# Moving squares, a copy and a norm check in a gated attention block: where they stand in the queues

## The chip, the core and the metric

The kernel runs on one core of one Trainium2 chip. The core has engines that each work through their own instructions in order: TensorE (PE in the profile; its weight loads are shown as PEld), VectorE (DVE), ScalarE (ACT), GpSimd (POOL) and SyncE (SP, which here only issues DMAs). They wait for one another through semaphores. The metric is the device time of one launch in microseconds (us); all times below are in us unless another unit is named.

## The reference

The input `x` is 32 batches of 256 rows of 256 values. Two blocks follow one another, each with a layer norm ahead of it and a gate behind it:

```
x = x + tanh(g_xattn) * xattn(layernorm(x), ctx, ctx)
x = x + tanh(g_ffn)   * ffn(layernorm(x))
```

`xattn` is an attention over 77 context rows with 8 heads, without a softmax over keys: it mixes cosine similarities with a term from variances, with weights that a small predictor computes once for the whole input. `ffn` is an attention of the 256 rows of a batch over themselves, with 16 heads, and two normalisations behind it:

```
scores = q k / sqrt(256)           (per head)
attn   = softmax(scores)
z = attn v ;  z = z @ Wo ;  z = z / max(|z|, 1e-12)
z = z @ Wff ; z = z / max(|z|, 1e-12) ;  z = gelu(z)
```

Where |z| isn't tiny, the first of the two normalisations falls out, since the second one divides by the length of every row anyway. The kernel uses that: it multiplies `Wo` and `Wff` once, and computes `u = z @ (Wo Wff)`, its rows' lengths, and gelu of the scaled rows.

## The kernel before

All arithmetic is in fp32. A preamble of about 130 us reads all of `x` once for sums over the whole input, turns the weights round and computes the predictor. Then one pass over the 32 batches follows.

**Order.** Every engine call goes through `InOrder` (line 24), which keeps the instructions of an engine in the order of the program. That order is written out by hand as lists of stages: `cycle` (line 1372), run once for each batch n from a little ahead of 0 up to 29, `last_but_one` (line 1443) for batch 30 and `last` (line 1483) for batch 31. An entry such as `(2, query_features, 0, 0)` runs that stage for batch n + 2, so a cycle works on up to seven batches at once: attention features for those ahead, the softmax of batch n, the output of batch n − 1. Two engines meet only in semaphores, which the framework sets from the tiles that are read and written. Two engines that read the same PSUM tile are ordered as well: the one that comes first in the program reads first. "Cycle n" below is the list's run for that n.

**The softmax of a batch.** It is done in four units u = 0 to 3, each of them in two halves.
- `scores(b, u)` (line 594): eight matmul instructions write scores into two PSUM buffers (pool `ps_s`, tile `sc`, two buffers, one for each half); VectorE then takes the negated maxima `nm`, one reduction for a half.
- `exponents(b, u, jp)` (line 625): four ScalarE activations for a half turn scores into `e` and add up rows into `sums`. Only then is that half's PSUM buffer free for the next unit's scores.
- `scale_values(b, u)` (line 637): VectorE takes the reciprocal of the sums and scales the values into `vz`.
- `mix_values(b, u)` (line 650): 16 matmul instructions multiply `e` and `vz` into PSUM tile `zp`. Behind unit 3, `zp` is copied to SBUF as `zT`, by VectorE (line 671). In batch 31 the copy is made in two parts, behind units 1 and 3 (line 668).

**The output of a batch.** It is done one cycle later.
- `ff_out(b)` (line 678): eight matmul instructions multiply `zT` by the joined weights into one PSUM tile of the pool `mm_tile` (line 141; three buffers, used in turn by nearly all other matmuls). ScalarE squares each half of it (tile `ge`) and adds up rows into `ny`; VectorE copies it to SBUF as `u`. In batch 31 each half has a PSUM tile of its own.
- `ff_keep` (line 704): two DMAs keep `zT` and `x` for a repair that is not needed on these inputs.
- `ff_norm_inv` (line 710): GpSimd turns `ny` into the reciprocal length `i2`.
- `ff_gelu`, `ff_add`: gelu, gate, and the DMA of the result. `ff_finish` (line 784) does all this at the end for batch 31.

**The check of the lengths.** `square_weights` (line 717) squares two weights on ScalarE, once, in cycle 4, into `bn`; its scratch tile has the tag `fb`, whose two buffers otherwise hold the transposed queries of `turn_queries` (line 470) until a DMA has read them. `bound_norms` (line 723), once, in cycle 5, sums `bn` over partitions on TensorE and makes the bound `low` of it on VectorE. `judge` (line 733), at the very end, compares all of `ny` with `low`; a repair loop, `mend`, would follow if a length were below it.

**Fillers.** `pass_time(b, n)` (line 189) issues n matmuls whose result nobody reads; the lists for the last two batches have some.

The stages around the change, as the list `cycle` has them before:

```
(-1, mix_values, 3), (0, scores, 0), ..., (0, exponents, 0, 0),
(-1, ff_out), (-1, ff_keep), (0, square_weights), (0, bound_norms),
(0, exponents, 0, 1), (2, query_features, 0, 0), (0, scale_values, 0),
(2, query_features, 0, 1), (-1, ff_norm_inv), (0, scores, 1), ...
```

Of the kernel before, what the change touches and what calls it, by code (L numbers as in the profile page):

```python
# [8 lines left out]
F32 = mybir.dt.float32  # L9
AF = mybir.ActivationFunctionType  # L10
# [4 lines left out]
P = 128  # L15
# [20 lines left out]
def gated_block_kernel(  # L36
# [25 lines left out]
    B, S, D = x.shape  # L62
    M = cx.shape[1]
    NT = S // P
# [6 lines left out]
    pa = ctx.enter_context(tc.tile_pool(name="pa", bufs=2))  # L71
# [7 lines left out]
    pe, act, dve, pool = (  # L79
        InOrder(tc, e) for e in (nc.tensor, nc.scalar, nc.vector, nc.gpsimd)  # L80
    )
# [36 lines left out]
    ny = const.tile([P, B, NT], F32, name="ny")  # L118
# [22 lines left out]
    def mm_tile():  # L141
        return ps.tile([P, 512], F32, tag="mm", name="mm")
# [60 lines left out]
    kept = [{} for _ in range(B)]  # L203
    given = set()

    def run(b, stage, *which):
        key = (b, stage.__name__, which)
        if key not in given:
            given.add(key)
            stage(b, *which)  # L210
# [439 lines left out]
    def mix_values(b, u):  # L650
        k = kept[b]
        g, kt = u // 2, u % 2
        if u == 0:
            k["zp"] = ps_z.tile([P, 2, S], F32, tag="zp", name="zp")
        es = [k.pop(("e", u, jp)) for jp in range(2)]
        for i in range(2):
            for j in range(4):
                pe.matmul(
                    k["zp"][32 * j : 32 * j + 32, g, :],
                    lhsT=vzs[u % 2][:, j, 2 * i : 2 * i + 2, :].rearrange("p i d -> p (i d)"),  # L660
                    rhs=es[j // 2][:, j % 2, i, :],
                    start=(i == 0 and kt == 0),
                    stop=(i == 1 and kt == NT - 1),
                )
        if b == B - 1 and u % 2:
            if u == 1:
                k["zT"] = pa.tile([P, 2, S], F32, tag="zT", name="zT", bufs=1)
            dve.tensor_copy(k["zT"][:, g, :], k["zp"][:, g, :])
        elif u == 3:
            zT = pa.tile([P, 2, S], F32, tag="zT", name="zT", bufs=1)  # L670
            dve.tensor_copy(zT, k.pop("zp"))
            k["zT"] = zT


# [3 lines left out]
    def ff_out(b):  # L678

        k = kept[b]  # L680
        pus = []
        for t in range(NT):
            if t == 0 or b == B - 1:
                pu = mm_tile()
            pus.append(pu[:, t * D : (t + 1) * D])
            for c in range(2):
                pe.matmul(
                    pus[t], lhsT=k["zT"][:, c, t * P : (t + 1) * P],
                    rhs=w_of[:, c, D : 2 * D], start=(c == 0), stop=(c == 1),
                )  # L690
        u = [P, NT, D], F32
        k["u"] = sw.tile(*u, tag="wf_n", name="u") if b == B - 1 else pa.tile(*u, tag="u", name="u")
        for t in range(NT):
            ge = pa.tile([P, D], F32, tag="ge", name="ge")
            act.activation(
                ge, pus[t], AF.Square, accum_out=ny[:, b, t : t + 1]
            )
        if b == B - 1:
            for t in range(NT):
                dve.tensor_copy(k["u"][:, t, :], pus[t])  # L700
        else:
            dve.tensor_copy(k["u"].rearrange("p t c -> p (t c)"), pu)

    def ff_keep(b):

        k = kept[b]
        nc.sync.dma_start(out=z_kept[:, b], in_=k["zT"])
        nc.sync.dma_start(out=x_kept[:, b], in_=k["x"])
# [12 lines left out]
                act.activation(ge, w, AF.Square, accum_out=bn[:, i : i + 1])  # L721

    def bound_norms(b):
        if b == 5:
            pt = mm_tile()
            pe.matmul(pt[:, 0:2], lhsT=ones, rhs=bn, start=True, stop=True)
            dve.tensor_copy(bn, pt[:, 0:2])
            dve.tensor_scalar(
                low, bn[:, 0:1], bn[:, 1:2], 4.0 * TINY * (S * D**0.5) ** 2, ALU.mult, ALU.mult
            )  # L730
            dve.tensor_scalar(low, low, LEAST, None, ALU.max)
# [388 lines left out]
    for g in range(NG):  # L1120
# [4 lines left out]
        for i in range(4):  # L1125
            k = 4 * g + i
# [233 lines left out]
    for pair in (2, 0, 1):  # L1360
# [11 lines left out]
    cycle = [  # L1372
        (4, load_queries),
        (-1, mix_values, 3),
        (0, scores, 0),
        (2, measure_keys),
        (2, align_keys),
        (3, norm_inputs),
        (0, exponents, 0, 0),
        (-1, ff_out),  # L1380
        (-1, ff_keep),
        (0, square_weights),
        (0, bound_norms),
        (0, exponents, 0, 1),
        (2, query_features, 0, 0),
        (0, scale_values, 0),
        (2, query_features, 0, 1),
        (-1, ff_norm_inv),
        (0, scores, 1),
        (0, exponents, 1, 0),  # L1390
        (0, mix_values, 0),
        (2, count_queries, 0),
        (2, query_features, 1, 0),
# [10 lines left out]
        (0, scores, 2),  # L1404
        (0, exponents, 2, 0),
        (0, mix_values, 1),
        (2, scale_keys),
        (1, attend, 0),
# [29 lines left out]
        (0, scale_values, 3),  # L1438
        (3, gain_inputs),
        (-1, ff_add),  # L1440
    ]

    last_but_one = [
        (-1, mix_values, 3),
        (0, scores, 0),
        (0, exponents, 0, 0),
        (-1, ff_out),
        (-1, ff_keep),
        (0, exponents, 0, 1),
        (0, scale_values, 0),  # L1450
        (1, query_ratios),
        (0, pass_time, 4),
# [36 lines left out]
        (0, exponents, 0, 0),  # L1489
        (0, exponents, 0, 1),  # L1490
        (-1, ff_out),
        (-1, ff_keep),
        (0, scores, 1, 1),
        (0, scale_values, 0),
# [14 lines left out]
        (0, exponents, 3, 0),  # L1509
        (0, mix_values, 2),  # L1510
        (0, pass_time, 5),
        (0, exponents, 3, 1),
        (0, scale_values, 3),
        (0, mix_values, 3),
# [51 lines left out]
```

## Time and profile before

| what | value |
|---|---|
| time, three runs | 1347.17, 1351.65, 1353.98 (median 1351.65) |
| the profiled execution's own time | 1349.24 |
| its span, first to last instruction | 1347.1 |
| TensorE busy | 1322.5 (98%) |
| VectorE busy | 1038.3 (77%) |
| ScalarE busy | 871.4 (65%) |
| GpSimd busy | 510.5 (38%) |
| mean granted TensorE clock | 0.997 |

A row of the timeline has the start, the duration, the engine, the line, the operation, the tiles (output <- inputs), their shape and the number of instructions merged into the row; in square brackets stands how long the engine was idle ahead of it and what ended that. The line is 32 everywhere, because all calls go through the helper `InOrder`, so one reads by the tiles' names: `sc` scores, `nm` maxima, `e` exponentials, `ge` squares, `zp` and `zT` the mixed values, `mm<-w_of,zT` the output product, `mm<-winT,xTc` query features, `vz` scaled values. A row of the waits has the engine and tile that waited, what it waited for, the total, the number of times and the longest. fp32 matmuls appear as two instructions each. The durations of matmuls are modelled and overlap, so the length of a run of matmuls is read from its start to the start of the next run.

### The profile page before, as it was taken

The numbers are of one execution on the slowest core, as the hardware profiler recorded it, in microseconds if no ns is written. First come the engines' busy times: TensorE is split into PE (matmuls) and PEld (weight loads), VectorE is DVE, ScalarE is ACT, GpSimd is POOL, SyncE is SP. The second block draws the span as 40 slices with busy tenths as digits, with TensorE's granted clock in tenths as the row PEclk, the third lists the DMA queues.
The fourth block names the chain that finished last, engine by engine and source line by source line (L and its number), as shares of the span: only waits on it lengthen the run. The fifth ranks groups of instructions, "written<-read, shape, count | busy, mean of one in ns | idle before, by whom it ended". The sixth has DMA issues, their size and how long they took to land.

```text
span 1347.1 us, 26283 instructions
## 1 busy us (share of the span) xinstructions
PE 1322.5 (98%) x8783; PEld 802.5 (60%) x8783; DVE 1038.3 (77%) x3004; ACT 871.4 (65%) x2857; POOL 510.5 (38%) x633
## 2 busy tenths in 40 slices
PE   8999999999999999999999999999999999999996
PEld 7866555666556556665556556665556565655563
DVE  6846778778788787787887787887887877878865
ACT  6822566766666767666666666666666676666666
POOL 6823344343333342435333433343433434343310
PEclk9999999999999999999999999999999999999999
DMA  8610033333233333332333333332333332422221
GB/s 275 208 32 21 28 97 116 110 115 93 70 118 113 106 116 105 117 108 88 86 114 110 115 108 116 108 101 88 101 113 106 120 101 89 134 84 68 80 86 41
DMA packets 99638, 138.25 MB, mean 103 GB/s; under 512 B 14170, under 2 KB 65039, under 8 KB 99502
## 3 DMA queue, kind: packets, MB, share of 16 engines
q1 hardware_dynamic: 98670, 136.56, 32.5%
q8 instruction: 70, 1.15, 0.3%
q14 instruction: 66, 0.54, 0.1%
q10 hardware_dynamic: 832, 0.00, 0.0%
HBM read 62.04 MB, written 64.23 MB: 94 GB/s over the span
## 4 chain that ended last, share of the span: by engine, by line
PE 91%; DVE 3%; DMA 2%; ACT 2%; POOL 1%; issue 1%; ACTq 0%; DVEq 0%; POOLq 0%; SPq 0%
PE mm L32 70%; PE sc L32 12%; PE zp L32 9%; ACT e L32 1%; DVE nm L32 1%; DMA x<-in_x_dram 1%; DMA ct<-in_ctx_dram 0%; DMA w_in_n<-in_L_xattn_w_in_dram 0%; POOL rstd_x L32 0%; DVE st L32 0%; DVE qt L32 0%; DVE qst L32 0%; DMA gcol<-in_L_xattn_ln_g_dram 0%; ACT ge L32 0%; POOL ct L32 0%
## 5 line engine op out<-in xcount | busy, mean ns | idle before, releaser
L32 ACT ACTIVATE e<-sc,nm 128x256 f32<-128x256 f32 x1016 | 467.5, 482 | 215.3 <-DVE nm L32 215.2
L32 DVE TENSOR_REDUCE nm<-sc 128x4 f32<-128x1024 f32 x254 | 298.6, 1216 | 42.8 <-PE sc L32 42.8
L32 PE MATMUL mm<-winT,xTc 128*128 128x512 f32 x512 | 234.9, 600 | 0.9 <-DVE bn L32 0.9
L32 ACT ACTIVATION_READ_ACCUMULATOR e<-sc,nm 128x1 f32 x1016 | 218.0, 215 | 0.0
L32 POOL TENSOR_TENSOR rq<-qt,nhalf 128x8 f32<-128x8 f32 x64 | 105.4, 1646 | 293.7 <-DVE qt L32 293.7
L32 PE MATMUL sc<-q,kTf 32*128 32x512 f32 x1016 | 164.0, 640 | 2.4 <-ACT e L32 1.4
L32 PEld LDWEIGHTS mm<-winT,xTc 128*128 128x128 f32 x512 | 94.0, 190 | 105.9 <-issue 102.2
L32 PE MATMUL mm<-vw,s 128*128 128x256 f32 x640 | 147.0, 384 | 0.0
L32 PE MATMUL zp<-e,vz 128*32 128x256 f32 x2048 | 137.0, 385 | 3.4 <-DVE vz L32 3.4
L32 PEld LDWEIGHTS mm<-vw,s 128*128 128x128 f32 x640 | 118.9, 190 | 28.8 <-issue 13.5
L32 POOL TENSOR_TENSOR fq<-fq,rq 128x1024 f32<-128x1024 f32 x64 | 121.4, 1896 | 5.0
L32 PEld LDWEIGHTS zp<-e,vz 128*32 128x32 f32 x2048 | 53.5, 109 | 107.5 <-issue 35.2
L32 POOL TENSOR_TENSOR nrx<-kt,nquart 128x8 f32<-128x8 f32 (+1 forms) x20 | 32.9, 1644 | 194.4 <-DVE kt L32 194.4
L32 DVE BATCH_NORM_STATS2 qst<-fq 128x6 f32<-128x128 f32 x512 | 104.6, 275 | 0.0
L32 PE MATMUL mm<-fqT,fvT 128*64 128x256 f32 (+2 forms) x1024 | 95.5, 387 | 0.0
L32 PE MATMUL mm<-woutT,fvT 128*64 128x256 f32 (+2 forms) x1024 | 93.7, 382 | 1.4 <-ACT v L32 1.4
L32 PEld LDWEIGHTS sc<-q,kTf 32*128 32x128 f32 x1016 | 48.2, 183 | 67.1 <-issue 41.0
L32 POOL TENSOR_SCALAR xn<-x,mv_x,rstd_x 128x256 f32<-128x256 f32 x64 | 80.2, 1261 | 4.2 <-issue 4.2
L32 ACT ACT_TABLE_LOAD x60 | 77.0, 1283 | 5.0 <-DMA x<-in_x_dram 4.3
L32 POOL TENSOR_SCALAR rs<-mv 128x1 f32<-128x1 f32 x64 | 14.4, 225 | 168.4 <-DVE mv L32 125.3
L32 ACT COPY fvx<-mm 128x512 f32<-128x512 f32 (+1 forms) x40 | 23.4, 585 | 80.3 <-PE mm L32 80.3
L32 PE MATMUL mm<-winT,kT_all 128*128 128x512 f32 (+1 forms) x160 | 74.9, 598 | 0.0
(232 smaller groups left out, 2160.6 us busy)
## 6 DMA issues: line engine op xcount, KB each, us to landing
fd<-fb SPq DMA_DIRECT2D x60, 512.0 KB
fqT<-fd SPq DMA_DIRECT2D x240, 128.0 KB
x<-in_x_dram SPq DMA_DIRECT2D x64, 256.0 KB
x_kept<-x SPq DMA_DIRECT2D x32, 256.0 KB
z_kept<-zT SPq DMA_DIRECT2D x32, 256.0 KB
out_dram<-x SPq DMA_DIRECT2D x31, 256.0 KB
xd<-xb SPq DMA_DIRECT2D x29, 256.0 KB
xq<-xd SPq DMA_DIRECT2D x116, 64.0 KB
```

The source lines that it names most:

```text
L32: return lambda *args, **kw: self._tc.keep_in_program_order(method(*args, **kw))
```

## The change

Five edits, four of them in the lists of stages:

1. The copy of `zp` to `zT` behind unit 3 is made by ScalarE instead of VectorE, in all batches but the last.
2. The squares of the output product are taken out of `ff_out` into a stage of their own, `ff_square`. In `cycle` and `last_but_one` it stands behind `exponents(0, 0, 1)` instead of ahead of it; in `last` it stands behind `ff_out`, where the squares were.
3. With that, VectorE's copy of the product to `u` comes ahead of the squares in the program (in batch 31 the squares stay ahead).
4. `square_weights` moves from the middle of cycle 4 to its end.
5. `bound_norms` moves from cycle 5 to the last batch, behind the second filler.

```diff
         elif u == 3:
             zT = pa.tile([P, 2, S], F32, tag="zT", name="zT", bufs=1)
-            dve.tensor_copy(zT, k.pop("zp"))
+            act.copy(zT, k.pop("zp"))
             k["zT"] = zT
...
-        for t in range(NT):
-            ge = pa.tile([P, D], F32, tag="ge", name="ge")
-            act.activation(
-                ge, pus[t], AF.Square, accum_out=ny[:, b, t : t + 1]
-            )
+        k["pus"] = pus
         if b == B - 1:
+            run(b, ff_square)
             for t in range(NT):
                 dve.tensor_copy(k["u"][:, t, :], pus[t])
         else:
             dve.tensor_copy(k["u"].rearrange("p t c -> p (t c)"), pu)
+
+    def ff_square(b):
+        for t, pu in enumerate(kept[b].pop("pus")):
+            ge = pa.tile([P, D], F32, tag="ge", name="ge")
+            act.activation(ge, pu, AF.Square, accum_out=ny[:, b, t : t + 1])
...
     def bound_norms(b):
-        if b == 5:
+        if b == B - 1:
...
         (0, exponents, 0, 0),
         (-1, ff_out),
         (-1, ff_keep),
-        (0, square_weights),
-        (0, bound_norms),
         (0, exponents, 0, 1),
+        (-1, ff_square),
         (2, query_features, 0, 0),
...
         (-1, ff_add),
+        (0, square_weights),
     ]
...
         (0, exponents, 0, 1),
+        (-1, ff_square),
         (0, scale_values, 0),
         (1, query_ratios),
...
         (-1, ff_out),
+        (-1, ff_square),
         (-1, ff_keep),
...
         (0, mix_values, 2),
         (0, pass_time, 5),
+        (0, bound_norms),
         (0, exponents, 3, 1),
         (0, scale_values, 3),
         (0, mix_values, 3),
```

## The prediction

> **What bounds the kernel now.** I read the page first: its span, its first part (busy time), its part 4 (the chain that ended last).
>
> ```profile
> span 1347.1 us, 26283 instructions
> PE 1322.5 (98%) x8783; PEld 802.5 (60%) x8783; DVE 1038.3 (77%) x3004; ACT 871.4 (65%) x2857; POOL 510.5 (38%) x633
> PE 91%; DVE 3%; DMA 2%; ACT 2%; POOL 1%; issue 1%; ACTq 0%; DVEq 0%; POOLq 0%; SPq 0%
> ```
>
> TensorE sets the end; VectorE at 77% and ScalarE at 65% have room. But a modelled busy row hides short stalls, because the modelled end of a matmul covers the wait behind it. So next I read who the weight loads (PEld) waited for: they can't start before what they wait for.
>
> ```profile
> PEld mm L32 <- DVE zT L32: 23.1, 31, 0.8
> PEld sc L32 <- ACT v L32: 12.4, 30, 0.4
> PEld sc L32 <- ACT e L32: 11.8, 31, 1.6
> ```
>
> Two of these are no stalls. After any run of eight score matmuls the loads pause 0.76, and after any mixing run 0.41, also where nothing is awaited. The third is one: score loads held, once a batch, by exponentials. The timeline of one cycle shows where:
>
> ```profile
> 601.84 1.14 PE L32 MATMUL sc<-q,kTf 32*128 32x512 f32 x8
> 602.00 0.69 DVE L32 COPY zT<-zp 128x512 f32<-128x512 f32 x1 [0.84 <-PE zp L32]
> 604.33 0.47 ACT L32 ACTIVATE e<-sc,nm 128x256 f32<-128x256 f32 x1 [2.79 <-DVE nm L32]
> 606.14 0.39 ACT L32 ACTIVATE ge<-mm 128x256 f32<-128x256 f32 x1
> 606.85 0.50 ACT L32 ACTIVATE e<-sc,nm 128x256 f32<-128x256 f32 x1
> 607.02 0.69 DVE L32 COPY u<-mm 128x512 f32<-128x512 f32 x1 [0.37 <-ACT ge L32]
> 608.20 0.52 ACT L32 ACTIVATE e<-sc,nm 128x256 f32<-128x256 f32 x1
> 608.27 1.72 PE L32 MATMUL sc<-q,kTf 32*128 32x512 f32 x8
> 608.86 0.30 PEld L32 LDWEIGHTS sc<-q,kTf 32*128 32x128 f32 x4 [0.30 <-ACT e L32]
> 609.92 1.07 PE L32 MATMUL zp<-e,vz 128*32 128x256 f32 x16
> ```
>
> The reader is to see: scores of unit 1 start at 608.27; their second half waits for the score buffer that the last exponential of unit 0 (608.20) frees. They hold TensorE until 609.92, 1.65, where the other score runs of the cycle take 1.07 (601.84 to 602.91, 617.86 to 618.93, 628.39 to 629.46). Two squares (606.14 to 606.85, 0.71) stand ahead of that last half. In all 27 ordinary cycles after the first the timeline gives 1.65 or 1.66; in the first cycle, which has no output product to square (148.75 to 149.82), 1.07. In cycle 4, where the weights' squares stand there too (299.43 to 300.66, 1.23), it is 300.85 to 303.72, 2.87: 1.22 more. So the run is late by just what stands ahead of the exponentials.
>
> **The change part by part.** Sums are against the profiled execution, 1349.24 (span 1347.1 and 2.1 around it), which is 2.4 under the median of the three runs, 1351.65.
>
> *Squares behind the second half.* The last exponential ends 0.71 earlier; the load at 608.86 could go at 608.15, before its run starts at 608.27, so the whole 0.58 is gone. 27 cycles × 0.585 = 15.8. Is the next step late? Unit 0's mixing needs the scaled values: their reciprocal starts at 608.84, now at 608.13, and the product ends 0.53 on, 608.66, against 609.34 where the mixing can start now. The output product's PSUM tile is held longer: its squares now end near 608.8. The third matmul group behind it reuses that tile, query features at 610.92, now 610.34: 1.5 of room. GpSimd's `i2` (610.50 in this cycle, behind its normalisations) gets its sums about 2 later at worst, and waits idle there in the others; its next task, `rq` at 616.19, came after 4.66 of idle. The copies of query features behind the squares start at 608.65 as before. Behind this point the other engines' work moves up with TensorE.
>
> *The order of the two readers.* VectorE's copy `u` waited for the squares (607.02, above; 28.6 in 32 waits). Now the copy is written first, so the squares wait for it; it ends near 607.4, squares start at 608.1: free. The Trainium skill, PSUM — Partial Sum Buffer, PSUM bank collisions raise a hardware error, says that ScalarE and VectorE must not read one bank together, so their reads have to be ordered; the trace agrees (607.02). If no order held, the next term would be nought. In the last batch ScalarE has no other work: copy 1323.05 to 1323.74, squares to 1324.5 instead of 1323.78, so the next exponentials start 0.7 late. Bounds: 0.7 lost, or 0.4 won, because VectorE's maxima move up from 1324.53 to 1324.1. ScalarE had 0.39 of idle at 1333.66 waiting for such a maximum; I follow the queue to there and take nought.
>
> *z copied by ScalarE.* VectorE's copy takes 0.69; ScalarE's copy of the same shape, `v<-mm`, 0.59. ScalarE's copy `v` ends at 601.54 and its next task starts at 604.33, so the new copy fits at 602.00 to 602.59, before the product's loads at 602.91. Queued behind it: those exponentials, not yet due. VectorE's maxima wait for scores (603.01) either way. Nothing on the path. In the last batch the copy ends about 1318.8 and the exponentials start there instead of 1318.46; 0.84 of idle at 1323.05 covers the 0.3.
>
> *Weights' squares at the end of cycle 4.* The 1.80 in that cycle (2.87 to 1.07) is gone. At the end `v` is copied until 333.08; squares take 1.23, and then the z copy 0.59: 334.90, for a product due at 334.45. Their scratch is the buffer of the transposed queries, read by DMAs issued at 328.98 and 330.11; the fetch behind the first started 2.67 later, so the second buffer is free by 332.8 to 333.5. Cost 0.5, bounds 0.4 and 1.2.
>
> *Norms' sum from cycle 5 to the last batch.* In cycle 5 it took a fourth PSUM tile, and query features waited: from the first scores to the second 333.38 to 341.22, 7.84, where it is 6.43 elsewhere. 1.41 gone (the 1.07 behind it stays; the 27 don't count this cycle). In the last batch the sum is queued on TensorE behind 10 filler matmuls, until 1337.51, and VectorE's three small operations behind it, ahead of unit 3's scaling, which before ran at 1335.63 and waited for nothing after. So: sum at about 1337.3, 0.3 to its end, 0.6 for the three (339.17 to 339.75), 0.6 from reciprocal to mixing: last mixing 1.5 late, less about 0.2 by which VectorE runs ahead. Cost 1.3; bounds 0.14 (the matmuls alone) and 1.7.
>
> *The cycle before the last.* Unit 1's scores took 2.92; 0.71 gone. A clock dip follows there, which the stretches show (TensorE's busy time, its clock behind POOL's):
>
> ```profile
> 1291.35:1294.76 3.41, 2.68 (x13) 0.76 (x13) 1.84 (x4) 2.19 (x11) 0.94 (x2) 1.00 0.18 67
> 1294.76:1298.17 3.41, 3.41 (x16) 1.59 (x16) 1.61 (x2) 1.57 (x6) 0.00 (x0) 0.50 0.02 5
> ```
>
> In it 16 matmuls of query scores took 3.55, elsewhere 1.88: 1.67. It is the only dip between 28 and 1346, and follows the stretch with the least work; with a shorter wait I expect it to go. Bounds 0 and 1.67; I take 1.67, as cycle 4's wait, nearly as long but followed by denser work, had no dip. The Trainium skill, TensorE: Matmul & The Clock Gate, Part 1, lets the clock drop after an idle window of about 3.4 us; the stretch ahead was busy for 2.68, so the trace differs. By that page the dip isn't tied to the wait and may stay: the sum would be 17.9.
>
> Sum: 15.8 + 1.8 − 0.5 + 1.4 − 1.3 + 0.7 + 1.7 = 19.6; 1349.2 − 19.6 = 1329.6. Three runs should lie somewhat above the profiled one, as before; half of the 2.4 makes 1331.
>
> **The rivals.**
>
> 1. *The wait moves to the PSUM tile.* If the squares end after 610.34, query features wait for the tile and part of the gain returns. For: cycle 5 shows that such a wait comes at once when a tile more is taken. Against: 1.5 of room, and nothing of VectorE's between. Half the 15.8 lost: 1339.
>
> 2. *The scores wait for something else* (a maximum's slot, a matmul), so the exchange does nothing steady. Against: 1.07 without squares, 1.22 more with 1.23 more. Only the single events remain, 1.4 net: 1348.
>
> 3. *The other side: z late on ScalarE.* It now stands at the head of ScalarE's queue before each output product. For: `q<-mm,par`, a ScalarE read of that shape, takes 0.71. Against: 0.71 still ends at 602.71. From 0.3 late TensorE waits; from 0.9 (an end at 603.5) it eats the 0.585. At 1.2 late, 29 × 0.3 = 9 slower: about 1359.
>
> 4. *The tail grows*: the last mixing 4 later instead of 1.3, for instance if a filler's tile is late too: 1334.
>
> **How the numbers follow.** Forecast 0.80, first rival 0.08, second 0.04, third 0.03, fourth 0.05. The range holds forecast and fourth rival. Down: best ends of the single events 1328, and the lowest run 2 under the profiled: 1326. Up: the dip stays, worst ends, 1333; a median 2.4 above and 2.3 of spread: 1338. About 0.5% is what a measurement of this kernel tells from no change; faster by more 0.93 (forecast, first and fourth), within 0.04, slower 0.03.
>
> **What would show it.** Unit 1's scores at 1.07 in every cycle and a cycle of about 37.2 instead of 37.74 (564.26 to 602.00, z copy to z copy); the PEld wait for `e` gone from 31 times to a few; no PEld wait on `fq` or `ge` in its place; the z copy on ScalarE ending before the product's loads; one wait of about 0.5 in cycle 5; the last mixing's loads waiting for `vz`, behind `bn`; no 0.50 clock before the end. Wrong if query features begin late behind 610, or the product's loads wait for zT by more than 0.76.

## The result, and the profile after

| | median | lowest to highest | runs |
|---|---|---|---|
| before | 1352.82 | 1347.17 to 1354.08 | 4 |
| after | 1332.51 | 1330.6 to 1335.0 | 4 |

The ratio is 0.9859, with a 95% interval of 0.9823 to 0.9895: faster by 1.4%. The forecast was 1331.0, with a range of 1326 to 1338. The profiled execution after took 1330.6 against 1349.24, 18.6 less, where the sum of the steps was 19.6.

The page of the changed kernel, by the same lines as before (span, busy time, the chain that ended last):

```profile
span 1328.6 us, 26302 instructions
PE 1303.1 (98%) x8783; PEld 793.6 (60%) x8783; DVE 1016.7 (77%) x2973; ACT 890.6 (67%) x2888; POOL 508.8 (38%) x633
PE 91%; DVE 3%; DMA 3%; POOL 1%; ACT 1%; issue 1%; SPq 0%; DVEq 0%; POOLq 0%; ACTq 0%
```

The shares hardly moved: TensorE is busy for 98% of the span and holds 91% of the chain, as before, and 19.4 of its modelled busy time is gone although it runs the same 8783 matmuls. Most of that time was a wait that the modelled ends covered; 1.67 of it was a stretch of half clock in the kernel before. VectorE lost 31 instructions and ScalarE won 31: the z copies.

One cycle in the timeline of the changed kernel (start, duration, engine, operation, tiles):

```profile
593.71 1.14 PE L32 MATMUL sc<-q,kTf 32*128 32x512 f32 x8
593.87 0.59 ACT L32 COPY zT<-zp 128x512 f32<-128x512 f32 x1 [0.46 <-PE zp L32]
594.78 1.99 PE L32 MATMUL mm<-w_of,zT 128*128 128x256 f32 x8
598.44 0.68 DVE L32 COPY u<-mm 128x512 f32<-128x512 f32 x1
599.37 0.50 ACT L32 ACTIVATE e<-sc,nm 128x256 f32<-128x256 f32 x1
599.82 0.42 ACT L32 ACTIVATE ge<-mm 128x256 f32<-128x256 f32 x1
600.14 1.14 PE L32 MATMUL sc<-q,kTf 32*128 32x512 f32 x8
600.23 0.29 DVE L32 TENSOR_TENSOR vz<-v,sums 128x128 f32<-128x128 f32 x1
601.21 1.07 PE L32 MATMUL zp<-e,vz 128*32 128x256 f32 x16
```

The reader is to see: the last exponential of unit 0 starts at 599.37, the first square only behind it at 599.82, and the scores of unit 1 take from 600.14 to 601.21, 1.07 instead of 1.65. The copy `u` (598.44) is done before the squares start. The z copy, now ScalarE's, ends at 594.46, before the product's loads. Unit 1's scores take 1.07 in every ordinary cycle, and 2.20 in the one before the last. In cycle 5 the first scores take 1.61, because z comes late there. From one z copy to the next (593.87 to 631.03) a cycle is 37.16, where it was 37.74.

A sign that was announced is missing, though. The waits of the weight loads in the changed kernel (total, times, longest):

```profile
PEld sc L32 <- ACT e L32: 23.7, 31, 1.2
PEld mm L32 <- ACT zT L32: 23.3, 30, 1.3
PEld sc L32 <- issue: 19.4, 65, 0.8
```

The wait for `e` still stands there 31 times, and longer in all than before (11.8). Yet the run of matmuls behind it is no longer late. Its 23.7 is about 31 × 0.76, the pause that the weight loads make after eight score matmuls in any case. Before, that pause stood in the row `issue`, which fell from 93 times to 65. The name moved because the exponential now ends inside the pause.

### The profile page after: what moved, and what is told of

It is laid out like the page before. It is cut to its first block, busy times and chain, and to the rows that moved or that the text cites. A ratio compares the mean times of both kernels' runs of the same rounds, so it can differ in the third digit from the quotient of the medians.

```text
span 1328.6 us, 26302 instructions
## 1 busy us (share of the span) xinstructions
PE 1303.1 (98%) x8783; PEld 793.6 (60%) x8783; DVE 1016.7 (77%) x2973; ACT 890.6 (67%) x2888; POOL 508.8 (38%) x633
## 4 chain that ended last, share of the span: by engine, by line
PE 91%; DVE 3%; DMA 3%; POOL 1%; ACT 1%; issue 1%; SPq 0%; DVEq 0%; POOLq 0%; ACTq 0%
PE mm L32 70%; PE sc L32 11%; PE zp L32 9%; DMA x<-in_x_dram 1%; DMA fd<-fb 1%; DVE nm L32 1%; DMA w_in_n<-in_L_xattn_w_in_dram 0%; DVE st L32 0%; ACT e L32 0%; DVE qt L32 0%; DVE qst L32 0%; POOL rstd_x L32 0%; DMA gcol<-in_L_xattn_ln_g_dram 0%; DVE fb L32 0%; SPq L504 0%
## 5 line engine op out<-in xcount | busy, mean ns | idle before, releaser
L32 PE MATMUL sc<-q,kTf 32*128 32x512 f32 x1016 | 147.1, 640 | 1.4 <-ACT kTf L32 1.0
L32 PEld LDWEIGHTS sc<-q,kTf 32*128 32x128 f32 x1016 | 40.2, 182 | 57.7 <-ACT e L32 23.7
```

The source lines that it names most:

```text
L32: return lambda *args, **kw: self._tc.keep_in_program_order(method(*args, **kw))
```

## The experiments

The kernel before was run again beside them: median 1349.59 (13 runs) beside the squares alone, all but the squares, the z copy put back and the first run with both checks placed; 1350.77 (one run) beside the three kernels with one run each; 1349.9 (11 runs) beside the rest.

The preamble differs from run to run: over the twelve profiled executions the first batch's output product starts at 180.79 to 183.79. So where 1 or 2 are at stake, the way from that product to the last batch's is compared. It takes 1156.25 in the kernel before and 1136.99 in the changed kernel.

### The squares alone, and all but the squares

The squares' move and the order of the two readers (edits 2 and 3) alone:

```diff
-            act.copy(zT, k.pop("zp"))
+            dve.tensor_copy(zT, k.pop("zp"))
...
-        if b == B - 1:
+        if b == 5:
...
         (-1, ff_keep),
+        (0, square_weights),
+        (0, bound_norms),
         (0, exponents, 0, 1),
...
         (-1, ff_add),
-        (0, square_weights),
...
         (0, pass_time, 5),
-        (0, bound_norms),
```

> Edits 2 and 3 alone: the squares stand behind the second half of exponentials and VectorE's copy u comes ahead of them; the z copy, the weights' squares and the norms' sum stay as before. Theory (the wait of unit 1's scores is just the ScalarE time ahead of the exponentials): 27 cycles at 1.07 instead of 1.65 (15.8 gone), cycle 4 at 2.16 instead of 2.87, the cycle before the last 0.7 less, and its clock dip gone (1.7). In cycle 5 the fourth PSUM tile now waits for squares that end later: the run of query features 5.8 instead of 4.80. Some 17.5 less than the profile of before: 1332. Rival (the z copy off VectorE brings the gain): scores stay at 1.65, time within 3 of before. Rival (the tile held): query features late in every cycle, 1339 or more.

Measured: 1333.15 (1327.79 to 1334.41), ratio 0.987 [0.9842, 0.9898]. Unit 1's scores take 1.07 in ordinary cycles and 2.14 in cycle 4, where the weights' squares still stand ahead. All of the gain that can be measured is here. One expectation failed: in cycle 5 the query features take 3.61 and nothing waits for a tile, although the norms' sum takes a fourth one; the run with later squares, below, explains that.

Edits 1, 4 and 5 without the squares' move:

```diff
         if b == B - 1:
-            run(b, ff_square)
...
+        run(b, ff_square)
+        if b == B - 1:
...
         (0, exponents, 0, 1),
-        (-1, ff_square),
```

(In all three lists the entry goes; the squares run inside `ff_out`, ahead of the copy `u`.)

> Edits 1, 4 and 5 without the squares' move: they stand between the two halves of exponentials, ahead of the copy u, as before. Theory: unit 1's scores keep 1.65 in the ordinary cycles, also in cycles 4 and 5 (2.87 and 1.07 before). Cycle 4 wins 1.2, cycle 5 1.4 less 0.6 less 0.5 for the weights' squares, the end loses 1.4: together nought, 1349 with the clock dip, 1347.5 without. Rival (the z copy on ScalarE brings the gain): 1.07, some 1332.

Measured: 1350.97 (1346.84 to 1354.3, 10 runs), ratio 1.0006 [0.9988, 1.0023]. Unit 1's scores take 1.66 or 1.67 in 28 cycles. So the other three edits together are worth less than 0.25% either way. The cycle before the last, in the timeline of this kernel:

```profile
1289.39 1.13 PE L32 MATMUL sc<-q,kTf 32*128 32x512 f32 x4
1291.26 1.13 PE L32 MATMUL sc<-q,kTf 32*128 32x512 f32 x4 [0.74 <-ACT e L32]
1292.32 2.93 PE L32 MATMUL mm<-fqT,fvT 128*64 128x256 f32 x32
```

From 1289.39 to 1292.32 the scores take 2.93, as long as before (2.92). And yet the query scores behind them run at full speed: their first 16 matmuls take 1.88, where the kernel before took 3.55 under a clock of 0.50. One row of the stretches (busy time of PE, PEld, DVE, ACT and POOL, then the clock, DMA share, GB/s):

```profile
1290.58:1294.00 3.42, 2.74 (x20) 1.36 (x20) 2.73 (x4) 1.18 (x6) 0.00 (x0) 1.00 0.02 5
```

The wait is there and the dip isn't. So the wait alone doesn't bring the dip, and the prediction's reason for its going, a shorter wait, isn't borne out. One execution can't tell whether a shorter wait makes the dip rarer.

### The z copy back on VectorE

```diff
-            act.copy(zT, k.pop("zp"))
+            dve.tensor_copy(zT, k.pop("zp"))
```

> The changed kernel with the z copy back on VectorE. Theory (that copy is off the path either way: VectorE waits for scores behind it, the product is due later): every run of matmuls of the cycles as in the changed kernel, only cycle 5 without the 0.5 in which z waited behind the weights' squares; some 0.5 less than the changed kernel, 1330. Rival (VectorE's 0.69 ahead of the maxima counts): up to 0.7 a cycle more, up to 1350.

Measured: 1332.36 (1328.56 to 1333.94), ratio 0.9867 [0.9844, 0.9891], against 0.9859 for all five edits. Up to the last batch, where this profiled execution had a stretch of half clock, the runs of matmuls are as long as in the changed kernel (within 0.3), with one exception that was expected: in cycle 5 the first scores take 1.07 instead of 1.61. Who makes this copy is of no account for the time, as the prediction had it.

### The squares split, the copy behind them, the squares later

Three kernels ask how much room the new order has. The first has one of the two squares ahead of the second half of the exponentials, and one behind:

```diff
+        (-1, ff_square, 0),
         (0, exponents, 0, 1),
-        (-1, ff_square),
+        (-1, ff_square, 1),
```

(`ff_square` takes the number of the half for this.)

> The changed kernel with one of the two squares back ahead of the second half of exponentials, the other behind. Theory (the wait is what stands ahead less the room): the second half of unit 1's scores could go 0.36 later than now, that is 0.23 late: the run takes 1.30 in the 29 cycles, 29 × 0.23 = 6.7 more than the changed kernel. Rival (a wait that comes with any square there, by the order of the readers): 1.65. Rival (all or nothing by the PSUM tile): 1.07. Here the first square also waits for VectorE's copy u, which ends about when the first half of exponentials ends or 0.7 later in cycles with key statistics; where it is later the wait grows to as much as 1.0.

Measured: 1355.19 in one run, more than in any of the 29 runs of the kernel before (at most 1354.33). Unit 1's scores take 1.29 in 10 cycles, as much as half of the squares' 0.71 would explain, but 2.42 or 2.43 in 17: a wait of 1.35, where 1.0 was expected at most. A cycle of each kind, the long one first, in the timeline of this kernel:

```profile
608.01 0.68 DVE L32 COPY u<-mm 128x512 f32<-128x512 f32 x1
608.73 0.38 ACT L32 ACTIVATE ge<-mm 128x256 f32<-128x256 f32 x1 [1.02 <-DVE u L32]
611.08 1.13 PE L32 MATMUL sc<-q,kTf 32*128 32x512 f32 x4 [0.24 <-ACT e L32]
...
645.24 0.68 DVE L32 COPY u<-mm 128x512 f32<-128x512 f32 x1
646.10 0.39 ACT L32 ACTIVATE ge<-mm 128x256 f32<-128x256 f32 x1
648.22 1.36 PE L32 MATMUL sc<-q,kTf 32*128 32x512 f32 x8
```

In the first kind ScalarE stood idle for 1.02 until VectorE had copied `u`, because VectorE first had its key statistics to do. All exponentials behind that square are late with it. In the second kind it had no such work, and nothing waits. Copy first (edit 3) thus costs nothing only while the squares stand far enough behind.

The second keeps the squares' new place, but the copy `u` comes behind them, as it did before the change:

```diff
-            dve.tensor_copy(k["u"].rearrange("p t c -> p (t c)"), pu)
+            k["pu"] = pu
...
             act.activation(ge, pu, AF.Square, accum_out=ny[:, b, t : t + 1])
+        if b < B - 1:
+            k = kept[b]
+            dve.tensor_copy(k["u"].rearrange("p t c -> p (t c)"), k.pop("pu"))
```

> The changed kernel with VectorE's copy u behind the squares again, as its second reader: the squares stand where the change put them. Theory: unit 1's scores keep 1.07, but VectorE stands waiting for the squares ahead of unit 0's scaling, so the first mixing comes about 0.8 late in each of 29 cycles: 23 more, 1354, no better than before. Rival (the order of the two readers doesn't matter): as the changed kernel.

Measured: 1354.66 in one run. Some 4.7 of it go with half clock in the last batch, of which more below (an estimate: that batch takes 5.1 more than in the changed kernel, and 0.4 of this is the order's). A cycle in the timeline:

```profile
607.90 0.43 ACT L32 ACTIVATE ge<-mm 128x256 f32<-128x256 f32 x1
608.46 0.69 DVE L32 COPY u<-mm 128x512 f32<-128x512 f32 x1 [2.19 <-ACT ge L32]
609.29 0.29 DVE L32 TENSOR_TENSOR vz<-v,sums 128x128 f32<-128x128 f32 x1
609.64 1.07 PE L32 MATMUL zp<-e,vz 128*32 128x256 f32 x16 [0.62 <-DVE vz L32]
```

VectorE waits 2.19 for the squares, and behind the copy stand the scaled values that mixing needs. From unit 1's scores to that mixing 28 cycles take 1.75 to 1.77, 0.69 more than in the changed kernel and 0.11 more than before; cycle 5 takes 1.18. That is 28 × 0.69 + 0.11 = 19.4 more than the changed kernel. Without the half clock it is about as slow as the kernel before: the squares' move without the exchange of the readers wins nothing. The exchange without the move was not run.

The third asks about the PSUM tile. The squares are put behind the first half of unit 1's exponentials, well past the 1.5 of room that the prediction gave:

```diff
         (0, exponents, 0, 1),
-        (-1, ff_square),
...
-        (-1, ff_norm_inv),
...
+        (-1, ff_square),
+        (-1, ff_norm_inv),
```

> The changed kernel with the squares (and the reciprocal length behind them) moved on behind the first half of unit 1's exponentials, some 4.5 later. Theory (the PSUM tile of the product has 1.5 of room): query features of the third group wait for that tile, 3.0 in each of 29 cycles: about 87 more, 1418. Rival (the tile isn't what query features take, or is free by the copy u alone): as the changed kernel.

Measured: 1332.8 in one run, as fast as the changed kernel, where 1418 was expected if query features waited for the tile. Its timeline:

```profile
600.92 3.70 PE L32 MATMUL mm<-winT,xTc 128*128 128x512 f32 x8
603.15 0.39 ACT L32 ACTIVATE ge<-mm 128x256 f32<-128x256 f32 x1
603.51 0.40 ACT L32 ACTIVATE ge<-mm 128x256 f32<-128x256 f32 x1
604.46 0.61 PE L32 MATMUL mm<-ident,qrp 128*128 128x128 f32 x4
```

The third group of query features starts at 600.92, while the squares read the product's tile from 603.15 to 603.9, and nothing waits. The PSUM addresses in the two built programs tell why. In the changed kernel two groups of query features have the two other banks, and the third group has the product's bank again. In this kernel the product has bank 0, the first two groups have banks 1 and 2, the third and fourth have 1 and 2 again, and bank 0 goes to the query ratios, needed at 604.46. This fits a pool that gives out the buffer whose last use comes first in the program, and not each in its turn: "used in turn", as it stands above, holds only while last uses come in the order of the takes. Cycle 5 in the run with the squares alone fits too: there the second group gets the bank of the norms' sum, and not that of the product.

### The two single events, and the clock

The changed kernel pays twice for the check of the lengths: 0.54 in cycle 5 and 1.4 in the last batch. Both can be placed better:

```diff
         (-1, ff_square),
+        (0, square_weights),
...
-        (0, square_weights),
...
-        (0, bound_norms),
         (0, exponents, 3, 1),
         (0, scale_values, 3),
+        (0, bound_norms),
```

> The changed kernel with the weights' squares straight behind the product's squares of cycle 4 (instead of its end), and the norms' sum in the last batch behind unit 3's scaling (instead of ahead of it). Theory: cycle 4 keeps 1.07 for unit 1's scores, since nothing is due on ScalarE there before 610 or so of the old time; the first scores of the next cycle take 1.07 instead of 1.61; the last mixing is no longer held by VectorE's three small operations, so 1.50 for the sum becomes about 0.15. 1.9 less than the changed kernel: 1328.7. Rival (the squares' copy of query features behind them is late): a wait of query features in cycle 4 of about 1.

Measured: 1332.32 (1331.52 to 1333.41), ratio 0.9876 [0.9857, 0.9895]; and the same kernel again in the last group:

> The kernel with both checks placed once more, beside the changed one and the one with fillers: by its runs of matmuls 1.9 less than the changed kernel in runs with the same dips; its fastest run about 1327, its median 1330 to 1332.

Measured: 1330.06 (1327.14 to 1332.24, 5 runs), ratio 0.9853 [0.9828, 0.9878]. In the profiled execution of the first, cycle 5's first scores take 1.07 and the sum's run 0.21 instead of 1.50, just as expected, and still its time is no better than the changed kernel's. The gain is there in the second, whose profiled execution has no half clock. From the first output product to the last it takes 1134.83, and a profiled execution of the changed kernel, also without half clock, takes 1136.72 in the run further below: 1.89 less, as expected. Its span is longer all the same, because its preamble was 2.71 longer. The tail of the second, in its timeline:

```profile
1315.96 0.20 DVE L32 RECIPROCAL sums<-sums 128x8 f32<-128x8 f32 x1 [1.97 <-ACT e L32]
1317.41 0.28 PE L32 MATMUL mm<-bn,ones 128*128 128x2 f32 x2
1317.62 1.07 PE L32 MATMUL zp<-e,vz 128*32 128x256 f32 x16
1317.72 0.16 DVE L32 COPY bn<-mm 128x2 f32<-128x2 f32 x1 [1.23 <-PE mm L32]
```

The scaling is ahead of the sum's small operations now, and the mixing (1317.62) no longer waits for them. What took the gain away in the first is seen in its stretches (columns as above):

```profile
1304.06:1307.47 3.41, 1.84 (x20) 0.72 (x20) 2.62 (x4) 3.41 (x17) 0.95 (x2) 1.00 0.01 2
1307.47:1310.88 3.41, 3.22 (x14) 0.91 (x16) 2.34 (x5) 3.41 (x17) 0.00 (x0) 0.50 0.00 0
1310.88:1314.30 3.42, 3.42 (x17) 1.01 (x10) 1.19 (x3) 2.65 (x12) 0.00 (x0) 0.50 0.00 0
1314.30:1317.71 3.41, 3.41 (x9) 2.22 (x8) 1.72 (x5) 2.26 (x9) 0.00 (x0) 0.50 0.02 5
```

In the last batch TensorE waits 1.75 for the scaled values `vz`, and then runs at half the clock for three stretches, 10.24. This costs 4.2 in the runs of matmuls, since part of that time TensorE would have waited anyway; one such stretch earlier, at 1256.27, makes its cycle 1.2 longer. The changed kernel's profiled execution has the same waiting stretch, but no dip behind it:

```profile
1303.04:1306.45 3.41, 1.66 (x26) 0.50 (x18) 3.00 (x5) 3.13 (x15) 0.94 (x2) 1.00 0.01 2
```

If the dip comes from that waiting, filler matmuls in it should keep it away. To the kernel with both checks placed, five were added:

```diff
         (0, exponents, 1, 1),
+        (0, pass_time, 3),
         (0, mix_values, 0),
...
         (0, exponents, 2, 1),
+        (0, pass_time, 2),
         (0, mix_values, 1),
```

> The kernel of the run with both checks placed, with three filler matmuls ahead of the first mixing and two ahead of the second mixing of the last batch, where TensorE waits for VectorE 1.8 and 0.9. Theory (half the clock is granted after a stretch in which the array did little, and whether a stretch boundary falls badly differs from run to run): with the gaps filled the dips of 10 in the last batch go, worth about 4 where they come: nearly all runs at 1327 to 1329, a median of 1328. Rival (the dips don't come from the gaps): the same spread as the changed kernel, 1327 to 1333. Rival (the fillers are in the way): the mixing later by up to 0.5 each.

Measured: 1329.03 (1328.18 to 1329.83), ratio 0.9846 [0.9819, 0.9872], with a mean clock of 0.998 in each of the four runs. The same part of its last batch, in stretches:

```profile
1301.86:1305.27 3.41, 2.83 (x19) 1.53 (x22) 2.87 (x5) 2.55 (x13) 0.94 (x2) 1.00 0.00 0
1305.27:1308.69 3.42, 3.40 (x26) 1.22 (x19) 1.99 (x4) 3.42 (x17) 0.00 (x0) 1.00 0.01 2
```

TensorE is busy for 2.83 instead of 1.84, and the clock stays. The fillers aren't free: from the first output product to the last this execution takes 1135.51, 0.68 more than the same kernel without fillers (1134.83), both without half clock in between. Beside it the changed kernel was run once more, as it is:

> The changed kernel once more, as it is, beside the others on one chip: 1329 to 1335, bimodal by the clock dip in the last batch; a median of 1332. If the prediction's step on the clock dip of the cycle before the last were right, no profile of it would show a dip there, and the runs would fall in two groups by the last batch alone.

Measured: 1334.15 (1328.57 to 1335.94, 6 runs), ratio 0.988 [0.9857, 0.9903]. Its runs fall into two groups: 1328.57 and 1329.96 with mean clocks of 0.999 and 0.997, and four from 1334.02 to 1335.94 with 0.992 to 0.994. Only the fastest of them was profiled, so where the others have their half clock isn't known. Over all runs of the kernels that have the squares in their new place, the copy `u` ahead of them, and no added fillers (27 runs: the changed kernel twice, the squares alone, z on VectorE, both checks placed twice), 8 have a mean clock of 0.997 or more; with the fillers 4 of 4 have. That speaks for the fillers, but four runs are few. The version with both checks placed and fillers has the lowest median: 5.1 under the changed kernel's in the same group, but only 1.0 under that of the same kernel without fillers, whose runs reach lower (1327.14). That the fillers pay is not shown.

## Why the prediction was right

**Squares behind the second half (15.8).** Right: 1.07 in place of 1.65 in 27 cycles, 0.58 each, 15.7. The kernel with the squares alone shows that edits 2 and 3 bring the gain, and the one without them that the other three edits bring none that can be measured.

**Order of the readers.** The order holds as told, and the copy first is free (0.68, over at 599.12, squares from 599.82). Its worth was passed over: the prediction gave no number for the old order beside the new place. It is 0.69 a cycle, more than the 0.58 that the move and the exchange win together. The Trainium skill, PSUM — Partial Sum Buffer, PSUM bank collisions raise a hardware error, asks that two engines don't read one bank together, and leaves open which reader goes first; here that decides 19.4. In the last batch the prediction took nought between 0.7 lost and 0.4 won: it is the best bound, 3.29 to 2.89 for the first run of scores, and 3.29 again in the kernel with the copy behind the squares.

**Z on ScalarE (nothing).** Right, shown by the copy put back: the same run lengths up to the last batch, but for cycle 5.

**Weights' squares (1.8 and −0.5).** Right: −1.80 in cycle 4, +0.54 in cycle 5. The timeline of the changed kernel at the start of cycle 5 shows the queue as foreseen, weights' squares ahead of the z copy:

```profile
329.22 0.65 ACT L32 ACTIVATE fb<-w_v 128x512 f32<-128x512 f32 x1
329.99 0.63 ACT L32 ACTIVATE fb<-w_of 128x512 f32<-128x512 f32 x1
330.62 0.57 ACT L32 COPY zT<-zp 128x512 f32<-128x512 f32 x1
331.24 1.99 PE L32 MATMUL mm<-w_of,zT 128*128 128x256 f32 x8 [0.47 <-ACT zT L32]
```

**Norms' sum (1.4 and −1.3).** Right in size: the sum's run (−0.14) and the query features (4.80 to 3.53) give −1.41. In the last batch the way to the last mixing is 1.40 longer. The chain is the one described, `bn` behind the fillers and the scaling behind `bn`, in the timeline of the changed kernel:

```profile
1316.56 0.28 PE L32 MATMUL mm<-bn,ones 128*128 128x2 f32 x2
1316.88 0.16 DVE L32 COPY bn<-mm 128x2 f32<-128x2 f32 x1 [3.73 <-PE mm L32]
1317.39 0.19 DVE L32 RECIPROCAL sums<-sums 128x8 f32<-128x8 f32 x1
1317.62 0.29 DVE L32 TENSOR_TENSOR vz<-v,sums 128x128 f32<-128x128 f32 x1
1318.06 1.07 PE L32 MATMUL zp<-e,vz 128*32 128x256 f32 x16 [1.22 <-DVE vz L32]
```

**The cycle before the last (0.7 and 1.7).** The size is right (2.92 to 2.20, and 3.55 to 1.88), but the second reason has no support: the kernel with all but the squares kept the wait and had no dip. Nor did the dip follow "the stretch with the least work": in the same profile 1322.06 to 1325.47 was busy for 2.02, with 13 matmuls as well, and had none behind it. Of the twelve profiled executions only the one that the prediction started from has a dip in this place, so the 1.67, nearly a tenth of the measured gain, was luck. Without it the forecast would lie 1.7 higher, still well inside the measured range. And "no 0.50 clock before the end" was fortunate as a sign: it holds in the profiled execution, but the mean clocks of other runs of the same kernel speak against it.

**The tile held longer (1.5 of room), and the first rival.** Nothing waited, as forecast, but the step behind it, "the third matmul group behind it reuses that tile", described only how the buffers fell in one order of the program. With the squares 4.6 later behind the product's start another buffer was handed out and nothing waited either. The rival's price of half the gain found no support.

**The sign `e` from 31 times to a few.** Wrong, as shown above: the prediction knew of the fixed pause of 0.76, and did not see that a wait which ends inside the pause keeps the name.

**Not foreseen.** Two small losses, less the 0.40 won in the last batch, make up about the difference between 19.6 and 18.6 (0.57 + 1.03 − 0.40 = 1.2). One is 0.57 in cycle 26, which the timeline of the changed kernel shows (SP's queue, then TensorE):

```profile
1124.97 4.11 SPq L504 DMA_DIRECT2D fqT<-fd  x8
1132.21 2.93 PE L32 MATMUL mm<-fqT,fvT 128*64 128x256 f32 x32 [0.49 <-DMA out_dram<-x]
```

and that of the kernel before does not:

```profile
1141.32 3.64 SPq L504 DMA_DIRECT2D fqT<-fd  x8
1148.54 2.93 PE L32 MATMUL mm<-fqT,fvT 128*64 128x256 f32 x32
```

The transposed queries for this cycle are fetched from DRAM late: the fetch starts 10.3 after the first DMA of their way out was issued, where 2.67 is usual. That happens at the end of cycles 5, 15 and 25 of both kernels (5.1, 8.9 and 10.3). Before, the last of these fetches was issued 4.02 ahead of the query scores, and now 3.56, because TensorE comes sooner: the matmul waits 0.49. The releaser that the row names had long been done; that it was the fetch follows from the order and was not tried in a run. It fits the other kernels: the run ahead of the query scores takes 0.53 or 0.54 in the four with cycles as long as before or longer, and 0.78 to 1.44 in the eight with short ones. The other is 1.0 after the last matmul: from its start to the end of the span it is 5.67, where it was 4.64. There the last DMAs are under way; why they end later stays open. Both differ between executions of one program: in the other profiled one of the changed kernel they are 0.31 and 0.47. The median, 1.5 above the forecast, has the clock in it: two of the four runs have mean clocks of 0.998, and two of 0.994 and 0.995.

## What to carry to other kernels

A matmul's modelled duration hides the wait for a free buffer; compare the same run of matmuls from start to start within a cycle, and look on the releasing engine's queue for work that nobody awaits soon. When such work is moved behind, see who else reads the same tile and has to wait for it: here the move won nothing without the exchange of copy and squares. Count a wait by the length of the runs and not by the rows of waits, since a fixed pause keeps the old name.

## What the runs showed of the hardware

In the pass over the batches the half clock comes in whole stretches of 3.41: one of them in the kernel before, three in a row (10.24) in the last batch of four others, one and two more in the kernel with the copy behind the squares. It mostly follows a stretch in which TensorE is little busy, but not always. Nine profiled executions have the squares moved, all or one of them, and no fillers added. Five of them have the dip in the last batch, behind a stretch with 1.54 to 1.84 of 3.41 busy, and four have none, behind 1.66, 1.67, 2.04 and 2.13. Elsewhere 2.68 was followed by it in the kernel before, and 2.74 wasn't in the one with all but the squares. Runs of one and the same kernel lie 4 to 7 apart (1328.57 and 1329.96 at mean clocks of 0.999 and 0.997, 1334.02 to 1335.94 at 0.992 to 0.994), about a third of what the change won, and the kernel before spreads likewise: 1346.78 at a clock of 1.0, 1354.33 at 0.993. The Trainium skill, TensorE: Matmul & The Clock Gate, Part 1, says that the window over which the clock is decided runs freely, isn't reset when a kernel starts, and is about 3.4 us long. The length agrees with these stretches, and a free-running window fits what is seen, that the same program has a mean clock of 0.999 in one run and of 0.992 in another; but the page asks for an idle window, and here TensorE was busy for 1.54 to 2.68 of it. How much work in a window is enough is not shown; modelled busy time alone doesn't decide it.
